# Second-layer softmax of a decoder stack: maxima subtracted by matmul, clamp on ScalarE, transposes by DMA

## The chip, the cores and the metric

The kernel runs on one core of one Trainium2 chip. A core has five engines with their own instruction streams: TensorE (PE in the profile, its weight loads PEld), VectorE (DVE), ScalarE (ACT), GpSimd (POOL) and SyncE (SP), which here issues all DMAs. TensorE writes to PSUM only[...]. The metric is the device time of one execution in microseconds (us), lower is better; "before" is the median of three runs.

## The reference

Four decoder layers run one after the other on 16 sequences of 128 tokens with 256 features, each with attention in 16 heads of 16 features and a feed-forward part. The first layer's attention works over features within a token, the other three over tokens. The second layer is the one whose attention changes; it quantizes queries, keys, values and the softmax weights to 8 bits:

```python
def _fq(x, delta, zp, n_bits):
    xi = _round_ste(x / delta) + zp
    xq = jnp.clip(xi, 0.0, 2.0 ** n_bits - 1.0)
    return (xq - zp) * delta
...
def _attn(x, ctx, wq, wk, wv, wo, bo, dq, dk, dv, dw):
    ...
    sim = jnp.einsum('bhid,bhjd->bhij', _fq(q, dq, 128.0, 8), _fq(k, dk, 128.0, 8)) * SCALE
    attn = jax.nn.softmax(sim, axis=-1)
    out = jnp.einsum('bhij,bhjd->bhid', _fq(attn, dw, 0.0, 8), _fq(v, dv, 128.0, 8))
    out = out.transpose(0, 2, 1, 3).reshape(b, n, D)
    return out @ wo + bo
```

The second layer runs this twice (on itself, then on the context), the third and fourth layers run plain softmax attention twice each:

```python
logits = jnp.einsum("bhqd,bhkd->bhqk", qh, kh) / jnp.sqrt(jnp.float32(depth))
if mask is not None:
    logits = logits + mask * -1000000000.0
attn = jax.nn.softmax(logits, axis=-1)
out = jnp.einsum("bhqk,bhkd->bhqd", attn, vh)
```

## The kernel before

**Tiling and order.** The 16 sequences are cut into 8 groups of two (`GB = 2`), and `group(g)` writes down all steps of all layers for one group. A step is one or a few instructions with the engines that may run them, a price for each, and the blocks that it reads and writes. `Plan.order` then lays all steps of all eight groups out in time by these prices, with all groups alive at once. It gives each block a place in one SBUF arena of 348 units of 512 bytes per partition, chooses the engine where a step has several ways, and emits the instructions in the order of the planned starts. `LEADS` holds one number per group and stage that is added to a step's due level and so sets which group goes first. The order on every engine, SP's queue of DMAs among them, is fixed by this: an instruction that waits holds up all that is behind it on its engine. PSUM is cut into four one-bank blocks (`pw`) and a single four-bank block (`ps`) for scores. Weights are loaded from DRAM by `weight` (L629) into the arena and are shared by the groups that meet them while they are there.

**The second layer's attention.** `quantized_attention` (L1045) makes integer-valued bf16 queries and keys (`qk`) and values (`vz`). `attention` (L886) then runs over the group's two sequences j. `begin(j)` (L1090) issues the scores of all 16 heads into `ps`: eight matmuls of 256 columns (helper line L833), with four 32-row strips of the array at a time. For each half c of the heads (eight heads), `soft` (L1097) then does:

- DVE takes the negated maximum of each row (L1099), and adds it to the scores on the way to SBUF (L1112); ACT takes the exponential in place (L1118). As a second way, which the planner may take, ACT reads PSUM head by head with the maximum as bias and sums on the way (L1103, L1105).
- DVE sums, inverts and scales (L1124 to L1127).
- POOL multiplies each of the eight heads by its factor and adds `MAGIC`, which rounds to a whole number (L1133); DVE clamps at 255, takes `MAGIC` off and writes bf16 (L1137).
- TensorE transposes the eight 128x128 blocks (L905) into PSUM, and ACT or DVE copies them to SBUF (L910, L911).

`out_of` (L1140) multiplies by the values with `products` (L867): 16 bf16 matmuls (L879), four 32-column strips at a time. ACT scales the result with `dwv` (L1143).

**The later layers' attention.** `plain_attention` (L1197) computes the scores twice: once with queries on the partitions, for the maxima only (L1236, or L1246 and L1251 where a mask is added), and once transposed (L1286, helper lines L844 and L833), so that the weights need no transpose. The negated maxima (16 a row, one a head) are split into three bf16 pieces by POOL or DVE (L1261 to L1264), laid into four 128x128 blocks `mq`, transposed by four PE transposes (L1271) and copied to SBUF (L1275). They enter the second scores by four matmuls of 512 columns with the constant `three`, which sums the three pieces (`below`, L1280, through `laid`, L841). Then 16 fp32 matmuls of 128 columns add the scores.

Of the kernel before, what the change touches and what calls it, by code (L numbers as in the profile page):

```python
# [66 lines left out]
SLOTS = {"sm": (64, 46), "row": (128, 12), "pw": (2048, 4), "ps": (8192, 1), "mq": (1024, 4)}  # L67
# [8 lines left out]
    [83, 27, 167, 130, 306, 193, 74, 226, 213, -45, 163, -53, 159, -84, 116, -64, 214, 400, 286, 283],  # L76
    [-69, -856, -114, -260, -60, 57, -165, -14, -2, -22, -386, -90, 144, -71, -260, -59, -586, -159, -213, -106],
    [49, -47, -11, 314, -162, 407, 51, 168, -361, -27, -172, 141, -4, -107, 36, 5, -54, 235, 78, 92],
    [-16, -228, 250, -173, -19, 106, 36, 203, -176, 14, 164, 2, 299, -144, 10, 309, -45, 154, 150, -1],
    [210, 166, 422, 222, 201, 790, 324, 499, 569, 334, 435, 116, 502, 205, 259, 760, 536, 716, 652, 178],  # L80
    [330, 158, 210, 147, 392, 517, 262, 488, 490, 57, 292, 77, 380, 208, 348, 38, 542, 447, 523, 1141],
    [267, 148, 130, 158, 333, 376, 220, 605, 204, -29, 43, 216, 340, 164, 196, 435, 324, 999, 754, 951],
    [288, 156, 593, 320, 407, 313, 255, 389, 233, 323, -30, 86, 440, 164, 213, 583, 372, 760, 452, 550],
# [344 lines left out]
def decoder_stack_kernel(ctx: ExitStack, tc: tile.TileContext, a: dict, out: bass.AP):  # L428
# [19 lines left out]
    G.memset(magic, MAGIC)  # L448

# [46 lines left out]
    three = const.tile([P, P], BF16, tag="three", name="three")  # L496
    mod = const.tile([P, 32], F32, tag="mod", name="mod")
# [28 lines left out]
    def prepare():  # L526
# [5 lines left out]
        def steps_of_quantization():  # L532
# [8 lines left out]
            V.tensor_tensor(dwv, d[:, :, 2], d[:, :, 3], ALU.mult)  # L541

# [6 lines left out]
        def masks():  # L549

            G.tensor_scalar(later[:, 0:1], mod[:, 0:1], -1.0, 1.0, ALU.mult, ALU.add)
            G.tensor_tensor(later[:, 1:2], later[:, 0:1], mod[:, 1:2], ALU.subtract)
            G.tensor_tensor(three, mod[:, 0:1].to_broadcast([P, P]), mod[:, 1:2].to_broadcast([P, P]), ALU.add)
            G.tensor_tensor(three, three, mod[:, 2:3].to_broadcast([P, P]), ALU.add)

            G.tensor_scalar(m1, m1, -1.0e9, 1.0, ALU.mult, ALU.mult)

        step([("POOL", 2.5, masks)], reads=[raw, dl_token], writes=[mask_token], least=110.0)


# [292 lines left out]
    def wide(v):  # L853
        return paired(v).unsqueeze(3).to_broadcast([P, 4, 2, S])

# [11 lines left out]
    def products(eTs, vz, j, po, ones=False):  # L867
# [3 lines left out]
        def issue():  # L871
            for c in range(2):
                for i in range(2):
                    for s in range(4):
                        if ones:
                            lhsT = ones2[:, i, :]
                        else:
                            lhsT = vz.ap()[:, j, 4 * c + s, 2 * i : 2 * i + 2, :].rearrange("p a d -> p (a d)")
                        T.matmul(  # L879
                            po.ap()[32 * s : 32 * s + 32, 2 * ones + c, :], lhsT=lhsT,  # L880
                            rhs=eTs[c].ap()[:, 2 * s + i, :], start=(i == 0), stop=(i == 1),
                        )
# [3 lines left out]
    def attention(x, wo, begin, soft, out_of, vz, dtype, after):  # L886


        plan.enter(after=after, w=1, oT=1, e=2, eT=2, **({"r": 1} if dtype == F32 else {"eb": 1}))
        wo = weight(wo)  # L890
        oT = block("m", [P, 2, NT], role="oT")
        for j in range(GB):
            ps, held = begin(j)
            eTs = []
            for c in range(2):
# [3 lines left out]
                per = 4 if dtype == F32 else 8  # L899
                for q0 in range(0, 8, per):  # L900
                    pt = block("pw", [P, per, S], dtype)

                    def turn(pt=pt, e=e, q0=q0):
                        for q in range(per):
                            T.transpose(pt.ap()[:, q, :], e.ap()[:, q0 + q, :], ident if dtype == F32 else ident_b)  # L905

                    step([("PE", 0.5, turn)], reads=[e], writes=[pt], holds=[eT])
                    step(
                        [
                            ("ACT", 0.6 if dtype == F32 else 1.2, lambda pt=pt, eT=eT, q0=q0: A.copy(eT.ap()[:, q0 : q0 + per, :], pt.ap())),  # L910
                            ("DVE", 0.66 if dtype == F32 else 0.7, lambda pt=pt, eT=eT, q0=q0: V.tensor_copy(eT.ap()[:, q0 : q0 + per, :], pt.ap())),  # L911
                        ],
                        reads=[pt], writes=[(eT, q0)],
                    )
# [130 lines left out]
    def quantized_attention(x, i, hT, kvT):  # L1045
# [44 lines left out]
        def begin(j):  # L1090
# [3 lines left out]
            step([("PE", 0.24, issue, "rows")], reads=[qk], writes=[ps], holds=es[:1])  # L1094
            return ps, es

        def soft(ps, j, c, e):  # L1097
            m, r, bias = small(8), small(8), small(8)
            step([("DVE", 1.22, lambda: V.tensor_reduce(paired(m.ap()), ps.ap()[:, :, c], AX.X, ALU.max, negate=True))], reads=[ps], writes=[m])  # L1099
            along = lambda: taken.eng == "ACT"  # L1100

            def per_head():
                A.activation(bias.ap(), m.ap(), AF.Copy, scale=one(sc))  # L1103
                for q in range(8):
                    A.activation(  # L1105
                        e.ap()[:, q, :], ps.ap()[:, q // 2, c, q % 2], AF.Exp, bias=bias.ap()[:, q : q + 1], scale=one(sc),
# [363 lines left out]
```

## Time and profile before

| | |
|---|---|
| median of 3 runs (lowest to highest) | 1461.03 us (1458.67 to 1462.03) |
| profiled execution | 1458.82 us, its span on the core 1456.7 us |
| granted TensorE clock, mean | 0.993 |
| DMA | 109.67 MB, 75 GB/s over the span |

The time of an execution is its span and some 2 us around it. The page gives for each engine the busy time and its share of the span, and then groups of instructions: source line, engine, operation, what is written and read, shape and count, then the busy time, the mean duration of one in ns, and the idle time of the engine just before them with what ended it. The line of a helper stands for all its callers, so `L833` and `L879` are told apart by shape and type. fp32 matmuls appear as two records each. Matmuls are pipelined: a record lasts longer than the step to the next one's start. The stage-by-stage lines are shown with the prediction; here are the groups of the step by step softmax of the second layer on DVE, ACT and POOL:

```profile
L1133 POOL TENSOR_SCALAR arena<-arena,sm 128x128 f32<-128x128 f32 x512 | 195.9, 403 | 107.7 <-DVE sm L1127 73.4
...
L1099 DVE TENSOR_REDUCE sm<-ps 128x8 f32<-128x1024 f32 x64 | 77.6, 1213 | 9.8 <-PE ps L833 9.5
...
L910 ACT COPY arena<-pw 128x1024 bf16<-128x1024 bf16 x56 | 56.3, 1011 | 41.9 <-PE pw L905 37.2
```

### The profile page before, as it was taken

Reading aid. Unit: us, or ns where it says so; the run is one execution under the profiler, and the core shown is the slowest. Engines: PE = TensorE matmul, PEld = TensorE weight load, DVE = VectorE, ACT = ScalarE, POOL = GpSimd, SP = SyncE. Lnnn points to the kernel's source line nnn. Section 1 sums busy time; section 2 is a strip of 40 time slices with the busy share of each in tenths; the row PEclk is TensorE's granted clock in tenths of the full one; section 3 lists DMA queues with packets and bytes.
Section 4 is the critical chain, followed back from the end, with each engine's and each line's share of the span. In section 5 each row is a group of like instructions: output and inputs, shape, how many; then the busy total and the mean of one; then the engine's idle time right before and its main releaser. Section 6 shows DMA issues by size and latency. Waiting matters only on the chain. (4 is left out here: it accounts for less than half of the span.)

```text
span 1456.7 us, 35756 instructions
## 1 busy us (share of the span) xinstructions
PE 1398.3 (96%) x14771; PEld 1141.3 (78%) x14771; DVE 1010.9 (69%) x1555; ACT 849.7 (58%) x1490; POOL 633.3 (43%) x1415
## 2 busy tenths in 40 slices
PE   8899998999899999899999999999999999999998
PEld 6677887878678888687878777777878888787777
DVE  1665788898988779767764976779478766556431
ACT  4565676766776656565554665657556454445552
POOL 2232857455777446524432542545634234243210
PEclk9999998999999999999999999999999999999999
DMA  6566513412432122112211532211210111100000
GB/s 207 138 171 192 188 48 102 117 34 67 125 90 95 44 67 70 56 52 66 84 38 45 160 101 97 85 55 56 73 45 2 42 38 66 31 31 2 2 9 23
DMA packets 138386, 109.67 MB, mean 75 GB/s; under 512 B 72288, under 2 KB 127472, under 8 KB 138096
## 3 DMA queue, kind: packets, MB, share of 16 engines
q1 hardware_dynamic: 138224, 107.40, 24.5%
q8 instruction: 116, 1.90, 0.5%
q14 instruction: 46, 0.38, 0.1%
HBM read 80.11 MB, written 27.26 MB: 74 GB/s over the span
## 5 line engine op out<-in xcount | busy, mean ns | idle before, releaser
L688 PE MATMUL pw<-arena 128*128 128x256 f32 x2048 | 484.2, 387 | 7.3 <-ACT arena L654 3.1
L675 PE MATMUL pw<-arena 128*128 128x256 f32 x2048 | 480.9, 385 | 7.8 <-ACT arena L663 2.5
L688 PEld LDWEIGHTS pw<-arena 128*128 128x128 f32 x2048 | 383.0, 192 | 68.8 <-issue 9.3
L675 PEld LDWEIGHTS pw<-arena 128*128 128x128 f32 x2048 | 379.2, 191 | 71.0 <-issue 10.0
L1133 POOL TENSOR_SCALAR arena<-arena,sm 128x128 f32<-128x128 f32 x512 | 195.9, 403 | 107.7 <-DVE sm L1127 73.4
L1314 DVE RECIPROCAL arena<-pw 128x256 f32<-128x256 f32 x64 | 112.1, 1752 | 104.0 <-PE pw L879 86.8
L734 POOL TENSOR_TENSOR arena<-arena,rows 128x512 f32<-128x512 f32 x107 | 137.7, 1289 | 89.7 <-ACT arena L721 74.0
L833 PE MATMUL ps<-arena 32*128 32x128 f32 (+2 forms) x3328 | 153.0, 309 | 2.8 <-DVE arena L1112 1.1
L1236 DVE TENSOR_REDUCE sm<-ps 128x16 f32<-128x2048 f32 x48 | 109.6, 2283 | 36.3 <-PE ps L833 33.8
L833 PEld LDWEIGHTS ps<-arena 32*128 32x128 f32 x3072 | 116.1, 186 | 20.4 <-issue 12.0
L696 DVE TENSOR_TENSOR arena<-pw,arena 128x512 f32<-128x512 f32 x88 | 60.3, 685 | 101.2 <-PE pw L688 99.7
L801 ACT ACTIVATE arena<-pw,cols_sb 128x256 f32<-128x256 f32 x184 | 78.0, 472 | 68.3 <-PE pw L675 65.5
L1261 POOL CAST mq<-sm 128x16 bf16<-128x16 f32 x58 | 15.8, 273 | 234.2 <-DVE sm L1236 114.6
L710 POOL TENSOR_SCALAR sm<-sm 128x2 f32<-128x2 f32 x88 | 20.6, 234 | 215.0 <-DVE sm L705 200.1
L721 ACT ACTIVATE arena<-arena,sm,sm 128x256 f32<-128x256 f32 x149 | 83.2, 597 | 49.3 <-POOL sm L714 48.7
L663 ACT ACTIVATE arena<-pw,cols_sb 128x256 f32<-128x256 f32 x140 | 72.7, 563 | 50.5 <-PE pw L647 47.0
L1275 ACT COPY arena<-pw 128x512 bf16<-128x512 bf16 x64 | 37.3, 582 | 84.5 <-PE pw L1271 77.6
L879 PE MATMUL pw<-arena 128*32 128x128 f32 (+1 forms) x2560 | 82.9, 265 | 3.4 <-ACT arena L910 3.0
L1099 DVE TENSOR_REDUCE sm<-ps 128x8 f32<-128x1024 f32 x64 | 77.6, 1213 | 9.8 <-PE ps L833 9.5
L1302 ACT ACTIVATE arena<-ps 128x1024 f32<-128x1024 f32 x64 | 64.1, 1025 | 33.1 <-PE ps L833 30.3
L647 PE MATMUL pw<-ident,arena 128*128 128x128 f32 x416 | 66.8, 286 | 15.1 <-DMA arena<-in_x_dram 5.1
L910 ACT COPY arena<-pw 128x1024 bf16<-128x1024 bf16 x56 | 56.3, 1011 | 41.9 <-PE pw L905 37.2
(142 smaller groups left out, 1993.8 us busy)
## 6 DMA issues: line engine op xcount, KB each, us to landing
arena<-in_L_xattn_ff_w_dram SPq DMA_DIRECT2D x38, 256.0 KB, 3.0
mha<-arena SPq DMA_DIRECT2D x16, 512.0 KB, 4.5
ca<-arena SPq DMA_DIRECT2D x16, 512.0 KB, 3.9
arena<-mha SPq DMA_DIRECT2D x16, 512.0 KB, 4.4
arena<-ca SPq DMA_DIRECT2D x16, 512.0 KB, 4.5
dqkv<-arena SPq DMA_DIRECT2D x8, 768.0 KB, 4.0
arena<-dqkv SPq DMA_DIRECT2D x16, 384.0 KB, 4.3
arena<-in_L_xattn_W_dram SPq DMA_DIRECT2D x24, 256.0 KB, 2.8
```

Of the source, the lines that this page charges most:

```text
L663: ("ACT", 0.54, lambda c=c: A.activation(dst.ap()[:, c, :], ps.ap()[:, c, :], AF.Identity, bias=biases(c), scale=scales(c))),
L675: T.matmul(ps.ap()[:, m, :], lhsT=w.ap()[:, k, m * P : (m + 1) * P], rhs=t.ap()[:, k, :], start=(k == 0), stop=(k == 1),)
L688: T.matmul(ps.ap()[:, j, :], lhsT=lhs(k, j) if lhs else t.ap()[:, k, j * S : (j + 1) * S], rhs=w.ap()[:, k, :], start=start and j + k == 0 ...
L721: ("ACT", 0.6, lambda j=j: A.activation(xh.ap()[:, j, :], x.ap()[:, j, :], AF.Identity, bias=nb.ap()[:, j : j + 1], scale=rstd.ap()[:, j : ...
L734: ("POOL", 1.33, lambda: G.tensor_tensor(dst.ap(), src.ap(), row(name), op)),
L801: "ACT", 0.47, lambda ps=ps, h=h, m=m, bias=bias: A.activation(h.ap()[:, m, :], ps.ap()[:, m, :], func, bias=bias),
L833: T.matmul(ps.ap()[:, s, c] if i is None else ps.ap()[:, s, c, i], lhsT=left(r, c) if i is None else left(r, c, i), rhs=right(r, c), start ...
L879: T.matmul(po.ap()[32 * s : 32 * s + 32, 2 * ones + c, :], lhsT=lhsT, rhs=eTs[c].ap()[:, 2 * s + i, :], start=(i == 0), stop=(i == 1),)
L1099: step([("DVE", 1.22, lambda: V.tensor_reduce(paired(m.ap()), ps.ap()[:, :, c], AX.X, ALU.max, negate=True))], reads=[ps], writes=[m])
L1133: G.tensor_scalar(e.ap()[:, q, :], e.ap()[:, q, :], r.ap()[:, q : q + 1], MAGIC, ALU.mult, ALU.add)
L1236: V.tensor_reduce(m.ap(), ps.ap().rearrange("p s c i k -> p (s c i) k"), AX.X, ALU.max, negate=True)
L1314: step([("DVE", 1.75, lambda po=po, r=r: V.reciprocal(r.ap(), po.ap()[:, 2:4, :]))], reads=[po], writes=[r])
```

## The change

In the second layer the maxima of all 16 heads are taken at once, split into three bf16 pieces, transposed and copied. Then the scores are computed a second time over a base that TensorE lays first: the transposed pieces times the constant `three_of`. ACT takes the exponential of half of this from PSUM in one instruction. After POOL's rounding, ACT computes `relu(MAGIC + 255 - e)`, which is 255 minus the clamped weight, as bf16. A DMA on SP's queue turns all eight blocks. `products` adds, for each weight block, a matmul with the constant `n255` (-255), so that the result is minus the wanted one, and `dwv` is negated. The alternative per-head way is gone.

For the later layers, `split` lays all pieces into one 128x128 block, `turned_maxima` transposes it once, and the copy is of 128 columns. In place of four 512-column matmuls, 16 of 128 columns (four heads f times four strips) stand among the score matmuls, with `three_of` picking head f's pieces. `LEADS` has other numbers, the `mq` slots are smaller, the sections' needs change (`mt=1`, `eb: 2`), and the constants are made at the start. The rest is as before.

```diff
-SLOTS = {... "mq": (1024, 4)}
+SLOTS = {... "mq": (256, 4)}
...
 LEADS = [
-    [83, 27, 167, 130, 306, 193, 74, 226, 213, -45, 163, -53, 159, -84, 116, -64, 214, 400, 286, 283],
+    [-105, -105, 449, 426, 143, 315, -548, 433, 727, -518, -25, 10, 121, -506, -369, -468, 179, -94, -43, -315],
...
+    top = const.tile([P, 1], F32, tag="top", name="top")
+    G.memset(top, MAGIC + 255.0)
+    n255 = const.tile([P, S], BF16, tag="n255", name="n255")
+    G.memset(n255, -255.0)
...
+            V.tensor_scalar(dwv, dwv, -1.0, None, ALU.mult)
...
+            for f in range(4):
+                t = three_of[:, f, :]
+                G.tensor_tensor(t, mod[:, 3 * f : 3 * f + 1].to_broadcast([P, P]), mod[:, 3 * f + 1 : 3 * f + 2].to_broadcast([P, P]), ALU.add)
+                G.tensor_tensor(t, t, mod[:, 3 * f + 2 : 3 * f + 3].to_broadcast([P, P]), ALU.add)
...
-        step([("POOL", 2.5, masks)], reads=[raw, dl_token], writes=[mask_token], least=110.0)
+        step([("POOL", 5.0, masks)], reads=[raw, dl_token], writes=[mask_token], least=75.0)
...
-    def products(eTs, vz, j, po, ones=False):
+    def products(eTs, vz, j, po, ones=False, missing=False):
...
+                    for n in range(1 if ones or not missing else 2):
+                        for s in range(4):
...
+                            T.matmul(
+                                po.ap()[32 * s : 32 * s + 32, 2 * ones + c, :], lhsT=lhsT,
+                                rhs=n255 if n else eTs[c].ap()[:, 2 * s + i, :], start=i == n == 0, stop=i == 1 and n == missing,
+                            )
...
     def attention(x, wo, begin, soft, out_of, vz, dtype, after):
-        plan.enter(after=after, w=1, oT=1, e=2, eT=2, **({"r": 1} if dtype == F32 else {"eb": 1}))
+        plan.enter(after=after, w=1, oT=1, mt=1, e=2, eT=2, **({"r": 1} if dtype == F32 else {"eb": 2}))
...
-                            T.transpose(pt.ap()[:, q, :], e.ap()[:, q0 + q, :], ident if dtype == F32 else ident_b)
-                    step([("PE", 0.5, turn)], reads=[e], writes=[pt], holds=[eT])
...
+                step(
+                    [("SP", 1.2, lambda e=e, eT=eT: nc.sync.dma_start_transpose(out=eT.ap(), in_=e.ap().rearrange("p q k -> p (q k)")), None, 1.0)],
+                    reads=[e], writes=[eT],
+                )
...
         def begin(j):
...
-            step([("PE", 0.24, issue, "rows")], reads=[qk], writes=[ps], holds=es[:1])
+            step([("PE", 0.24, issue, "rows")], reads=[qk], writes=[ps])
+            m, rest, mq = small(16), small(16), block("mq", [P, P], BF16)
+            step(
+                [("DVE", 2.3, lambda ps=ps: V.tensor_reduce(m.ap(), ps.ap().rearrange("p s c i k -> p (s c i) k"), AX.X, ALU.max, negate=True))],
+                reads=[ps], writes=[m],
+            )
+            mt = turned_maxima(m, rest, mq)
+            def less(ps):
+                for s in range(4):
+                    T.matmul(
+                        ps[:, s].rearrange("p c i k -> p (c i k)"), lhsT=mt.ap()[strip(s)],
+                        rhs=three_of[strip(s)].rearrange("p f k -> p (f k)"), start=True, stop=False,
+                    )
+            ps, issue = scores(less, lambda r, c: qT(r, c, tok), lambda r, c: kz(r, c, tok), True)
+            step([("PE", 0.46, issue, "rows")], reads=[qk, mt, mask_token], writes=[ps], holds=es[:1])
...
         def soft(ps, j, c, e):
...
+                [("ACT", 1.15, lambda: A.activation(paired(e.ap()), ps.ap()[:, :, c], AF.Exp, scale=one(sc)), "exp")],
...
-            step([("DVE", 0.76, lambda: V.tensor_scalar(eb.ap(), e.ap(), MAGIC + 255.0, -MAGIC, ALU.min, ALU.add))], reads=[e], writes=[eb])
+            step([("ACT", 1.05, lambda: A.activation(eb.ap(), e.ap(), AF.Relu, bias=top, scale=-1.0))], reads=[e], writes=[eb])
...
+    def turned_maxima(m, rest, mq):
+        def split(eng):
+            piece = lambda n: mq.ap().rearrange("p (s r) -> p s r", r=32)[:, :, 0:12].rearrange("p s (f n) -> p s f n", n=3)[:, :, :, n]
+            four = lambda t: t.ap().rearrange("p (s f) -> p s f", f=4)
+            eng.tensor_copy(piece(0), four(m))
+            eng.tensor_tensor(four(rest), four(m), piece(0), ALU.subtract)
+            eng.tensor_copy(piece(1), four(rest))
+            eng.tensor_tensor(piece(2), four(rest), piece(1), ALU.subtract)
+        step([("DVE", 1.0, lambda: split(V)), ("POOL", 1.25, lambda: split(G))], reads=[m], writes=[rest, mq])
+        pt, mt = block("pw", [P, S], BF16), block("m", [P, S], BF16, role="mt")
+        step([("PE", 0.1, lambda: T.transpose(pt.ap(), mq.ap(), ident_b))], reads=[mq], writes=[pt], holds=[mt])
+        step(
+            [("ACT", 0.32, lambda: A.copy(mt.ap(), pt.ap())), ("DVE", 0.25, lambda: V.tensor_copy(mt.ap(), pt.ap()))],
+            reads=[pt], writes=[mt],
+        )
+        return mt
...
+            mt = turned_maxima(m, rest, mq)
...
+                for f in range(4):
+                    c, i = divmod(f, 2)
+                    for part in (0, 1) if i else (1, 0):
+                        for s in range(4):
+                            r = strip(s)
+                            T.matmul(
+                                pT.ap()[:, s, c, i], lhsT=kz.ap()[r, c, i, tok] if part else three_of[r, f, :],
+                                rhs=qT.ap()[r, c, tok] if part else mt.ap()[r],
+                                start=masked_T is None and part == 1 - i, stop=(f == 3 or masked_T is None) and part == i,
+                            )
```

## The prediction

> **What bounds the kernel now.** I read the busy shares first, then the stretches in time, then the TensorE groups, then who waits for whom.
>
> ```profile
> span 1456.7 us, 35756 instructions
> PE 1398.3 (96%) x14771; PEld 1141.3 (78%) x14771; DVE 1010.9 (69%) x1555; ACT 849.7 (58%) x1490; POOL 633.3 (43%) x1415
> ```
>
> TensorE (PE) is busy for 96% of the span. Matmuls overlap, so this alone proves little; what does is how long it stands still. In stretches of 100 us (columns: length, then busy time and count of PE, PEld, DVE, ACT, POOL, then clock and DMA):
>
> ```profile
> 0.00:100.00 100.00, 84.99 (x685) 70.64 (x686) 43.09 (x108) 56.89 (x133) 27.56 (x55) 0.98 0.63 173
> ...
> 300.00:400.00 100.00, 94.12 (x1075) 77.16 (x1074) 89.54 (x149) 66.67 (x128) 60.47 (x136) 0.98 0.26 80
> ...
> 700.00:800.00 100.00, 97.70 (x1228) 80.97 (x1227) 62.23 (x92) 52.69 (x84) 37.37 (x83) 1.00 0.16 53
> ...
> 1100.00:1200.00 100.00, 99.72 (x1208) 82.71 (x1210) 75.59 (x90) 57.08 (x96) 30.61 (x72) 1.00 0.09 28
> ```
>
> After the first 100 us PE never rests for more than 7 us in 100, and the granted clock is full (0.993 in the mean). DVE comes near a bound only between 200 and 600 us (85 to 90%). The end is thus set by the amount of matmul work; a faster DVE or ACT is worth only some of the 58 us for which PE is idle in all (15 in the first 100 us, 22 between 100 and 600). No long wait of PE is for a weight DMA: the only DMA waits are 7.9 us for x and the context at the start. The groups which the change touches (busy us, mean ns, idle before):
>
> ```profile
> L905 PE MATMUL pw<-ident_b,arena 128*128 128x128 bf16 x512 | 40.2, 222 | 5.2 <-DVE arena L1137 2.6 <-DVE arena L1315 1.1 <-ACT arena L1058 0.9
> L844 PE MATMUL ps<-arena,three 32*128 32x512 bf16 x320 | 31.6, 384 | 2.5 <-DVE sm L1236 2.2 <-ACT arena L1302 0.2
> L1271 PE MATMUL pw<-ident_b,mq 128*128 128x128 bf16 x256 | 25.1, 220 | 2.4 <-DVE mq L1264 1.7 <-POOL mq L1264 0.7
> L879 PE MATMUL pw<-arena 128*32 128x128 bf16 x512 | 13.8, 222 | 3.2 <-ACT arena L910 3.0
> L833 PE MATMUL ps<-arena 32*128 32x256 bf16 x256 | 12.7, 272 | 1.8 <-DVE arena L1112 1.1 <-POOL arena L1068 0.4 <-ACT arena L1302 0.3
> ```
>
> Means of 220 to 384 ns are latencies. What a matmul takes from PE is the time from its start to the next one's start; summed over the trace these are 39.4 us for L905 (77 ns each), 18.8 for L1271 (0.294 us per four), 0.226 us per four of `three`, 18.5 for the bf16 L879 (every fourth 56 ns, the others 3 to 4, since four strips run together), 11.4 for the bf16 L833 (0.356 us per eight). These, not the means, are my prices.
>
> **PE, part by part.** There are 32 batches in the second layer (8 groups, 2 attentions, 2 sequences) and 64 in the two later layers.
>
> - Turns of the weights by DMA: 512 transposes go, -39.4 us.
> - Maxima of the later layers in one transpose: three of four go. A group of four took 0.294, less 3 x 0.056 (the step within a group) leaves 0.126 for one: 64 x 0.126 - 18.8 = -10.7 us.
> - The second layer gains such a transpose: 32 x 0.126 = +4.0 us.
> - Its second scores: four matmuls of 512 columns (0.226) and eight of 256 (0.356): 32 x 0.582 = +18.6 us.
> - Products with `n255`: 16 more matmuls, four rounds of 0.056: 32 x 0.224 = +7.2 us.
> - Later layers: four 512-column matmuls become 16 of 128 columns among the fp32 ones. The trace has no such mixture. Rounds of four fp32 scores start 111 ns apart, with weight loads of 187 ns under way meanwhile; bf16 ones of 128 columns 56 ns apart. Two of the four new rounds come just before an fp32 weight load, which I let set their pace: 2 x 0.056 + 2 x 0.107 = 0.32 us against 0.226, so 64 x 0.096 = +6.1 us. Low end: no extra. High end: each of three additional changes of operand type costs the 0.2 us seen from the last score (903.241 us) to the next full-width matmul (903.441), +38 us. I stay near the low end, since the one change of type in the trace is free: last `three` matmul at 902.236, first fp32 score 217 ns later, just its 512 columns:
>
> ```profile
> 902.23 0.39 PE L844 MATMUL ps<-arena,three 32*128 32x512 bf16 x4
> 902.45 1.06 PE L833 MATMUL ps<-arena 32*128 32x128 f32 x32
> ```
>
> Sum: -39.4 - 10.7 + 4.0 + 18.6 + 7.2 + 6.1 = **-14.2 us** of PE work.
>
> **The other engines.** DVE loses, per half batch, one subtraction (61 x 1.22), the clamp (64 x 0.78) and 8 copies of 0.68; its 64 reductions of 1.21 become 32 of 2.28 (equal), and 11 more splits of 1.47 and a few row additions and diagonal steps fall to it: about -107 us, from 69% to 63%. ACT loses the copies (56.3), the exps from SBUF (69.1), the per-head form (16.5) and 37.3 at L1275; it gains 64 exps from PSUM at 1.11 (the L1302 row with a bias column), 64 Relus at about 1.1 and 90 copies of 128 columns at about 0.27 (from 376 ns for 256 and 582 for 512): about -15 us. POOL gets 21 more splits of 1.06 us and loses seven larger steps: about +6. All these lie beside PE. Their worth is in the 22 us of PE idle between 100 and 600 us; I take **-4 us**, since most of these waits are short and of many kinds.
>
> Here the Trainium skill speaks against one edit: "ScalarE: Activation LUTs", Rules for kernel authors, wants relu, max and min on VectorE. By the rows the clamp costs 0.78 us on DVE and about 1.1 on ACT, so the rule is right for the step alone: 64 x 0.3 = 20 us more engine time. But neither engine sets the end, and DVE is the fuller one where PE idles; by rule or row the sum stays as it is.
>
> **The new chain and its waits.** First scores, reduction 2.28, split 1.06, transpose, copy 0.27, second scores: some 4 us in which PE's next step for this batch waits, and behind it everything in PE's fixed order. The later layers already run exactly this chain; their L1271 waited 2.4 us in 64 batches, so 32 more cost +1.2 us. After the second scores: exp 1.11, sum, reciprocal and scale 1.69, POOL twice 8 x 0.403 (L1133), Relu 1.1: 10.3 us, then the turn. In the built order of PE, other work priced as above stands between a batch's second scores and its products: 18 us in the tightest case, 24 in the next, about 56 in the middle. A landing of up to 8 us is hidden everywhere, one of 14 in all but one case. I add 1 us.
>
> **The turn by DMA** is not in the trace. Nearest rows: loads of the same 256 KB.
>
> ```profile
> arena<-in_L_xattn_ff_w_dram SPq DMA_DIRECT2D x38, 256.0 KB, 3.0
> arena<-in_L_xattn_mha_wv_dram SPq DMA_DIRECT2D x6, 256.0 KB, 4.0
> ```
>
> They hold SP for 0.4 us. Low end 3 us. High end from the skill: "VectorE: DVE Perf Modes", The three transpose paths, gives 390 ns on TensorE and 1309 ns by DMA for 128x128 bf16, and its rules prefer TensorE where PSUM will do. Eight blocks would be 10.5 us, an estimate from that page; held on SP for all of it, 64 x 10.5 = 670 us of queue. The trace's TensorE price is 77 ns, so by the rule this is the worse path by far. I take about 4.5 us to land and 1 to 2 on SP, nearer the row, because that page's figure is for a lone block and its fixed part need not recur eight times. What matters is whose time it is: PE is the bound and is spared 39 us, while SP has room, 382 records at 0.43 = 164 us of issuing in the span. In the built order SP gets 64 turns and 17 fewer weight loads. A turn waits for its Relu, and weight loads queued behind it wait too; SP already stands in waits up to 90 us long without PE ever waiting for a weight, so I cost this at nothing. If that cover goes, the rival below is what happens.
>
> **Sum:** 1458.8 (profiled execution, span 1456.7 and 2.1 around it) - 14.2 - 4 + 1.2 + 1 = 1442.8, say **1442 us**. The median of the three runs, 1461.0, is 2 us above the profiled execution; the forecast is 1.3% below it.
>
> **Rivals.**
> 1. *The order packs better as well* (chance 0.14). PE waits over 0.5 us add up to 46 us, 15 of them in the first 60 us; with DVE down, half of the rest goes: 1442 - 15 = 1427. For it: DVE at 86 to 90% just where PE rests. Against: the waits have over twenty different releasers, DVE's clamp (L1137) alone 2.6 us.
> 2. *PE saves nothing* (0.06): the interleaved fp32 and bf16 scores cost 0.22 us per batch more than priced, 64 x 0.22 = +14: 1442 + 14 = 1456, no change. The free change of type above speaks against it.
> 3. *The turns choke the queue* (0.20), the slower side. Place: SP, between the first and last turn (150 to 1100 us in the old trace), one turn in 15 us. At 10.5 us each they take 670 of 950 us, other issues 105; the remaining 175 must hold all waits for slots and inputs, which today are far more. Weight loads then miss their matmuls: 1.5 us for each pair of turns (most of the 1.9 us step that a weight feeds) gives 32 x 1.5 = 48: 1442 + 48 = 1490. It decides from about 6 us of SP per turn, half of what lies between two turns. For it: fixed order, one queue for all. Against: 3 us rows, and weights that today are never late.
>
> **How the numbers follow.** Forecast 0.60, own range 1430 to 1452 (the score rounds at +0 or +14, idle better or worse by 8). With rival 1 that makes faster 0.74; rival 2 is within 0.2%, about what a measurement of this kernel can tell from no change; rival 3 slower, 0.20. The range of 1424 to 1466 holds the forecast, most of rival 1, rival 2 and the mild end of rival 3.
>
> **What would show it.** PE: no 128x128 bf16 group of 512; about 14 us less start-to-start time, the interleaved rounds near 0.32 us of bf16 per batch. DVE near 63%. The turn: landing near 4.5 us, SP held below 2. No PE or PEld wait put down to weights or turned tiles. Wrong if turns land beyond 10 us, if PE waits for weight DMAs add up to over 10 us, or if PE idle grows from 58 us by more than the work that is saved.

## The result and the profile after

The changed kernel takes 1466.30 us (median of 7 runs, 1465.19 to 1468.25), the kernel before in its 7 runs 1461.03 (1457.88 to 1462.34). The ratio is 1.0048 with a 95% interval of 1.0037 to 1.0059: the change makes it slower by half a per cent, where 1442 us was forecast.

The head of the page after the change, as the first fence of the prediction showed it before:

```profile
span 1465.5 us, 37787 instructions
PE 1403.0 (96%) x15763; PEld 1137.2 (78%) x15763; DVE 898.5 (61%) x1455; ACT 832.6 (57%) x1483; POOL 615.7 (42%) x1502
```

VectorE is rid of 112 us, ScalarE of 17. TensorE, the bound, is busy for 4.7 us longer, in 992 more matmuls, and the span is 8.8 us longer. Stretches of 100 us after the change (length, busy time and count of PE, PEld, DVE, ACT, POOL, then granted clock and DMA):

```profile
200.00:300.00 100.00, 84.98 (x745) 66.60 (x744) 69.03 (x128) 70.50 (x122) 73.55 (x177) 0.91 0.39 100
300.00:400.00 100.00, 96.62 (x856) 76.79 (x855) 67.50 (x123) 66.96 (x119) 60.97 (x158) 0.99 0.48 118
...
600.00:700.00 100.00, 89.65 (x1185) 69.55 (x1185) 71.18 (x107) 54.07 (x90) 51.16 (x130) 0.97 0.30 68
700.00:800.00 100.00, 99.76 (x1164) 81.53 (x1163) 62.99 (x93) 54.18 (x91) 46.09 (x106) 1.00 0.38 112
```

and two of them before it:

```profile
200.00:300.00 100.00, 93.69 (x729) 76.50 (x729) 85.99 (x144) 72.75 (x138) 61.56 (x137) 0.95 0.34 91
...
600.00:700.00 100.00, 97.61 (x1117) 79.47 (x1110) 66.93 (x90) 58.56 (x87) 32.11 (x77) 1.00 0.17 54
```

VectorE is at 67 to 69% between 200 and 400 us, where it was at 86 to 90%. Yet PE stands still for 15.0 us between 200 and 300 us (6.3 before) and for 10.4 between 600 and 700 (2.4 before), and the clock is lower just there: 0.91 against 0.95, and 0.97 against 1.00. In most other stretches PE rests less than before. The rests have moved to other places. GpSimd is fuller there than it was (74% for 62, and 51 for 32), VectorE a little in the second stretch (71% for 67), but no engine beside PE is near full in either.

To compare kernels I split each span in three. **Idle** is the span less PE's busy time, both on the page. **Half clock** is what PE loses while busy in stretches in which the trace grants it a clock of 0.50 (counted as half of its busy time there). **Work** is the rest: busy time at full clock.

| us | span | work | idle | half clock |
|---|---|---|---|---|
| before | 1456.7 | 1389.2 | 58.3 | 9.1 |
| after | 1465.5 | 1386.2 | 62.5 | 16.7 |
| difference | +8.8 | -3.0 | +4.2 | +7.6 |
| in the prediction | -16.0 | -14.2 | -1.8 | 0 |

So there are three errors to explain: 11 us of work that did not go, 6 us of idle time, and 8 us of half clock, a term that the prediction did not have at all.

**Where half clock comes from.** PE's timeline near 278 us (start, duration, then in brackets the idle time before), and the clock in the stretches around:

```profile
269.41 1.06 PE L1017 MATMUL pw<-arena 128*32 128x128 f32 x32
...
277.98 0.62 PE L844 MATMUL ps<-arena 32*128 32x256 bf16 x8 [5.79 <-ACT arena L1114]
...
280.37 1.94 PE L1017 MATMUL pw<-arena 128*32 128x128 f32 x32 [0.73 <-ACT arena L665]
```

```profile
272.00:278.00 6.00, 0.20 (x5) 0.11 (x6) 4.88 (x11) 5.46 (x10) 3.38 (x6) 0.80 0.38 58
278.00:282.40 4.40, 3.67 (x57) 2.71 (x60) 4.23 (x8) 2.17 (x3) 4.16 (x12) 0.50 0.33 61
282.40:290.00 7.60, 7.60 (x75) 6.19 (x66) 6.50 (x15) 6.63 (x12) 6.45 (x20) 1.00 0.34 54
```

PE waits 5.8 us for the exponential that frees the one block of PSUM for scores. What ScalarE does meanwhile, in its own fixed order:

```profile
273.03 1.11 ACT L1114 ACTIVATE arena<-ps,sc 128x1024 f32<-128x1024 f32 x1
274.65 1.09 ACT L732 ACTIVATE arena<-arena,sm,sm 128x256 f32<-128x256 f32 x2 [0.51 <-POOL sm L725]
275.65 1.13 ACT L1133 ACTIVATE arena<-arena,top 128x1024 bf16<-128x1024 f32 x1
276.81 1.11 ACT L1114 ACTIVATE arena<-ps,sc 128x1024 f32<-128x1024 f32 x1
```

Between the exponentials of the two halves stand a normalization and the Relu of another step; this Relu, 1.1 us, is work that the change gave to ScalarE. In the last part of PE's wait the clock drops to half, and it stays there until 282.4 us: the same 32 matmuls of L1017 take 1.94 us in place of 1.06. Within the span, the trace has four such stretches before the change (three of 3.4 us, one of 10.2) and eight after it (3.4 or 6.8 us), besides one at the very end, where PE has nothing left to do. The Trainium skill ("TensorE: Matmul & The Clock Gate", Part 1) says that a monitor looks at windows of about 3.4 us and halves the clock after an idle one, and its table under "Why this matters for your kernels" wants no gaps of PE above about 3 us. The lengths agree. The bound is too mild for this case: of the eight stretches, seven follow 3.4 us in which PE was busy for 26 to 52% (the eighth follows 3.4 us without work), and the longest waits just before or at their start are 2.0 to 5.8 us, five of them below 3. By the rule three waits of the changed kernel would cost half clock; by the trace eight do, and they cost the 16.7 us. Nor is the share of busy time alone the rule: before the change PE was busy for 46% of the 3.4 us from 842.4 us on, and kept the full clock.

### The profile page after: what moved, and what is told of

Same layout as the page of the kernel before. It is cut to its first block, busy times and chain, and to the rows that moved or that the text cites. A ratio compares the mean times of both kernels' runs of the same rounds, so it can differ in the third digit from the quotient of the medians.

```text
span 1465.5 us, 37787 instructions
## 1 busy us (share of the span) xinstructions
PE 1403.0 (96%) x15763; PEld 1137.2 (78%) x15763; DVE 898.5 (61%) x1455; ACT 832.6 (57%) x1483; POOL 615.7 (42%) x1502
## 4 chain that ended last, share of the span: by engine, by line
PE 86%; DVE 6%; ACT 5%; issue 2%; POOL 1%; DMA 0%; SPq 0%; ACTq 0%; DVEq 0%; POOLq 0%
PE pw L686 29%; PE pw L699 29%; PE pw L889 8%; PE ps L1287 6%; PE ps L844 5%; PE pw L658 3%; PE ps L855 2%; DVE sm L1253 1%; ACT arena L960 1%; ACT arena L1308 1%; DVE sm L1119 1%; PE pw L984 1%; POOL arena L1128 1%; DVE sm L1095 1%; PE pw L1017 1%
## 5 line engine op out<-in xcount | busy, mean ns | idle before, releaser
L1128 POOL TENSOR_SCALAR arena<-arena,sm 128x128 f32<-128x128 f32 x512 | 188.9, 391 | 60.5 <-DVE sm L1122 33.6
L745 POOL TENSOR_TENSOR arena<-arena,rows 128x512 f32<-128x512 f32 x103 | 131.3, 1276 | 95.4 <-ACT arena L732 78.1
L1150 POOL CAST mq<-sm 128x16 bf16<-128x16 f32 x79 | 19.2, 243 | 295.3 <-DVE sm L1095 112.2
L1253 DVE TENSOR_REDUCE sm<-ps 128x16 f32<-128x2048 f32 x48 | 109.7, 2284 | 48.2 <-PE ps L844 48.0
L844 PE MATMUL ps<-arena 32*128 32x256 f32 (+1 forms) x1536 | 97.9, 356 | 9.7 <-ACT arena L1114 5.8
L1287 PE MATMUL ps<-arena 32*128 32x128 f32 x2048 | 97.2, 298 | 2.0 <-DVE sm L1253 1.0
L1119 DVE TENSOR_REDUCE sm<-arena 128x8 f32<-128x1024 f32 x64 | 77.5, 1211 | 31.5 <-ACT arena L1114 30.7
L1287 PEld LDWEIGHTS ps<-arena 32*128 32x128 f32 x2048 | 75.7, 187 | 23.5 <-issue 16.6
L889 PE MATMUL pw<-arena 128*32 128x128 f32 (+1 forms) x2560 | 89.0, 267 | 4.7 <-ACT arena L793 3.8
L1133 ACT ACTIVATE arena<-arena,top 128x1024 bf16<-128x1024 f32 x64 | 73.5, 1149 | 31.3 <-POOL arena L1128 25.8
L721 POOL TENSOR_SCALAR sm<-sm 128x2 f32<-128x2 f32 x88 | 17.7, 201 | 174.2 <-DVE sm L716 170.7
L1095 DVE TENSOR_REDUCE sm<-ps 128x16 f32<-128x2048 f32 x32 | 73.0, 2282 | 15.9 <-PE ps L844 15.5
```

The lines of the kernel that those rows point to most:

```text
L745: ("POOL", 1.33, lambda: G.tensor_tensor(dst.ap(), src.ap(), row(name), op)),
L844: T.matmul(ps.ap()[:, s, c] if i is None else ps.ap()[:, s, c, i], lhsT=left(r, c) if i is None else left(r, c, i), rhs=right(r, c), start ...
L889: T.matmul(po.ap()[32 * s : 32 * s + 32, 2 * ones + c, :], lhsT=lhsT, rhs=n255 if n else eTs[c].ap()[:, 2 * s + i, :], start=i == n == 0, ...
L1095: [("DVE", 2.3, lambda ps=ps: V.tensor_reduce(m.ap(), ps.ap().rearrange("p s c i k -> p (s c i) k"), AX.X, ALU.max, negate=True))],
L1119: V.tensor_reduce(r.ap(), e.ap(), AX.X, ALU.add)
L1128: G.tensor_scalar(e.ap()[:, q, :], e.ap()[:, q, :], r.ap()[:, q : q + 1], MAGIC, ALU.mult, ALU.add)
```

## The experiments

All ratios are to the kernel before, timed on the same chip in the same rounds.

**1. The small products issued together.** In the later layers the change puts 128-column bf16 products among the fp32 scores. This version issues the 16 bf16 ones first and the 32 fp32 ones after them:

```diff
-                for f in range(4):
-                    c, i = divmod(f, 2)
-                    for part in (0, 1) if i else (1, 0):
+                for part in (0, 1):
+                    for f in range(4):
+                        c, i = divmod(f, 2)
...
-                                start=masked_T is None and part == 1 - i, stop=(f == 3 or masked_T is None) and part == i,
+                                start=masked_T is None and part == 0 and f == 0, stop=f == 3 and part == 1,
```

> The changed kernel, with the 16 three_of matmuls of a later layer's second scores issued first and the 32 fp32 records after them, nothing else moved on any engine. Work theory (the mixture costs PE time): the block of second scores takes 1.43 us from its start to the next step in the changed kernel and 1.22 in the one before; grouped it falls to about 1.21, 64 x 0.22 = 14 us less, so about 1452 us, ratio 0.994 to the kernel before. Waiting theory (the loss is in waits for the score block and the half clock after them): the time that is freed goes into waits, under 4 us gained, about 1463. Order theory (the planned order itself is worse): the same, about 1463.

Measured: 1459.24 us (1458.04 to 1462.69), ratio 0.9995 (0.9985 to 1.0004). The timeline of one batch in the changed kernel:

```profile
658.25 0.50 PE L1287 MATMUL ps<-arena 32*128 32x128 f32 x8
658.58 0.29 PE L1287 MATMUL ps<-arena,three_of 32*128 32x128 bf16 x8
658.69 0.68 PE L1287 MATMUL ps<-arena 32*128 32x128 f32 x16
659.19 0.29 PE L1287 MATMUL ps<-arena,three_of 32*128 32x128 bf16 x8
659.30 0.46 PE L1287 MATMUL ps<-arena 32*128 32x128 f32 x8
```

and in this version:

```profile
657.13 0.40 PE L1287 MATMUL ps<-arena,three_of 32*128 32x128 bf16 x16
657.37 1.12 PE L1287 MATMUL ps<-arena 32*128 32x128 f32 x32
658.41 1.08 PE L889 MATMUL pw<-arena 128*32 128x128 f32 x32
```

Read the starts; a round is four records, one for each strip of the array. By the medians over the 62 batches at full clock, an fp32 round starts 0.111 us after the one before it and a bf16 round 0.056. Two kinds of round take longer: the fp32 round that begins the block (0.214 us to the next start), and the first fp32 round behind each pair of bf16 rounds (0.165). In the lines this is 0.33 us for the first two fp32 rounds (x8) in place of 0.22, and 0.50 for the four in the middle in place of 0.44. The step from fp32 to bf16 costs nothing extra (0.111). In the kernel before, the first fp32 round stands behind products of 512 columns and takes 0.109; in this version, behind four bf16 rounds, 0.165. From the start of a block to the next step's start, the medians over 64 batches are 1216 ns before the change (226 for the four 512-column matmuls, 990 for the scores), 1434 after it and 1279 here. Interleaving costs 64 x 0.218 = 14.0 us of PE, grouping 64 x 0.063 = 4.0. Grouping does not reach the 1.21 us that was expected of it, so 10 us could go and not 14: the work falls by 9.1 us against the changed kernel (1386.2 to 1377.1), the time by 7.1.

**2. Only the turns by DMA.** The kernel before with the DMA turn in place of transposes and copies, a second eb block, and `LEADS` as they were:

```diff
-                            T.transpose(pt.ap()[:, q, :], e.ap()[:, q0 + q, :], ident if dtype == F32 else ident_b)
...
+                    [("SP", 1.2, lambda e=e, eT=eT: nc.sync.dma_start_transpose(out=eT.ap(), in_=e.ap().rearrange("p q k -> p (q k)")), None, 1.0)],
```

> The kernel before with one part of the change alone: the weights are turned by DMA (two eb blocks, as in the change), all else and LEADS as before. Work theory: the 64 turns took 0.457 us each at full clock, 29 us of PE work goes and nothing comes in its place, so about 1432 us, ratio 0.980; turns land in about 3.1 us as in the changed kernel. Queue theory (turns on SP hold up weights): 1461 or slower, with PE waits put down to weight DMAs.

Measured: 1550.35 us, ratio 1.0611 (1.0594 to 1.0628), with work 1359.0, idle 148.1 and half clock 41.7. PE's work falls by 30.2 us, and the time rises by 90. The turn's own line in this run (min/median/max ns on the queue, then who waited for it):

```profile
L900 SPq DMA_TRANSPOSE arena<-arena x64: 1231/1233/3332, 148.2 to 1242.5; - x64
...
  PE pw L879: 18.9, 6
...
DMA to landing us min/median/max: 3.0/3.1/6.6
```

A turn holds the queue for 1.23 us and lands after 3.1, and still PE waits 18.9 us for turned tiles, six times. The longest of these waits, 8.3 us, ends with a turn that was issued 0.03 us after VectorE had made its input, which was late; the next, 6.9 us, with one that left 2.6 us after its input was there, behind loads, and took 6.6 to land. No wait of PE is for a weight, so the queue theory, which wanted waits for weights, fell too. The remaining idle time has many other names, such as 12.2 us of score steps waiting for L1100 on VectorE. The gain was there, and idle time and half clock together took four times as much (89.8 and 32.6 us more than before).

**3. Turns by DMA, one transpose for the pieces, small products grouped.** The previous one with the change's `turned_maxima` and `three_of` in the later layers; in the second layer the maxima are still subtracted by DVE (60 of 64 half batches) or ACT. `LEADS` is that of the kernel before.

> As e2_turns, and the later layers' maxima in one transpose with the three_of matmuls grouped ahead of the fp32 ones; the second layer keeps its subtraction on VectorE and its clamp on VectorE. Work theory: 29 us of turns and 64 x (0.234 - 0.066) = 11 us of transposes go, the grouped matmuls cost nothing more: about 1421 us, ratio 0.973. Waiting theory: less than half of this, 1441 or slower, since freed PE time turns into waits. Order theory: nothing said about its sign, as LEADS were not made for it.

Measured: 1517.61 us, ratio 1.0390 (1.0374 to 1.0406), with work 1351.4, idle 127.0, half clock 38.9. This is the least work so far, 37.8 us below the kernel before, in a kernel 4% slower. What the changed kernel does beyond this, above all the second scores and the products with `n255`, takes the saving back: its work is 1386.2.

**4. The changed kernel with the old `LEADS`.** Nothing but the table goes back.

> The changed kernel with LEADS of the kernel before, so another order of the same work. Order theory (the new LEADS are the loss): faster than the changed kernel, 1458 or less, ratio under 1.0. Work and waiting theories: the same PE work in an order not made for it, 1470 to 1490, ratio 1.006 to 1.02.

Measured: 1544.78 us, ratio 1.0575 (1.0557 to 1.0594), with work 1391.6, idle 112.1, half clock 39.1. Against the changed kernel only the planner's order differs, and 78 us with it; neither theory had so much. With the order goes the choice of engine where a step has several ways, since the planner makes both; "order" means both from here on. Every comparison of one edit under a table made for something else (2, 3 and 4) measures first of all the table.

**5. and 6. A shorter hold of the score block, and as much relief elsewhere.** PE waits 22.0 us ahead of steps that write the score block, 5.5 before the change. If VectorE's maxima (2.28 us each) hold it too long, halving them should help, and the same relief at other places should not. The first version takes the maxima of 64 of the 96 batches over half of the columns; the second leaves those whole, and takes the second layer's sums and the statistics of the normalizations over half (the last two cuts below).

```diff
-                [("DVE", 2.3, lambda ps=ps: V.tensor_reduce(m.ap(), ps.ap().rearrange("p s c i k -> p (s c i) k"), AX.X, ALU.max, negate=True))],
+                [("DVE", 2.3, lambda ps=ps: V.tensor_reduce(m.ap(), ps.ap().rearrange("p s c i k -> p (s c i) k")[:, :, 0:64], AX.X, ALU.max, negate=True))],
...
-                    V.tensor_reduce(m.ap(), ps.ap().rearrange("p s c i k -> p (s c i) k"), AX.X, ALU.max, negate=True)
+                    k = S if may_be_empty else 64
+                    V.tensor_reduce(m.ap(), ps.ap().rearrange("p s c i k -> p (s c i) k")[:, :, 0:k], AX.X, ALU.max, negate=True)
...
-                V.bn_stats(st.ap()[:, j, :], x.ap()[:, j, :])
+                V.bn_stats(st.ap()[:, j, :], x.ap()[:, j, 0:128])
...
-                V.tensor_reduce(r.ap(), e.ap(), AX.X, ALU.add)
+                V.tensor_reduce(r.ap(), e.ap()[:, :, 0:64], AX.X, ALU.add)
```

> The changed kernel; 64 of the 96 reductions of maxima (all of the second layer's, and those of the two context attentions of the later layers) look at half of each row's columns, so some maxima are not the true ones. Same order on every engine. Each reduction holds the score block ps about 1.1 us less, 64 x 1.1 = 70 us less of DVE and of the block's 840 us. Score-block theory (PE waits because the one block is not free): PE's idle time before score steps falls from 22 us to under 15, and the kernel gains 8 us or more, 1458 or less. Rival (DVE and the chain as a whole are late, whatever they hold): it gains no more than e7_half_elsewhere.

> The changed kernel; the second layer's 64 sums of exponentials and the 176 row statistics of the norms look at half of the columns, so sums and norms are not the true ones. Same order on every engine. About 64 x 0.6 + 176 x 0.13 = 61 us less of DVE, none of it while the score block is held. Score-block theory: PE's idle time before score steps stays above 17 us, and the gain is under 4 us, 1462 or more. Rival (chain as a whole is late): it gains as much as e6_half_maxima or more.

Measured: 1465.27 us, ratio 1.0037 (1.0024 to 1.0050), and 1463.25, ratio 1.0021 (1.0009 to 1.0033). VectorE is down by 64 and 51 us, the waits ahead of the score block still 19.3 and 20.5 us, the time lower by 1 to 3 us in both. The theory fell: neither VectorE's hold of the block nor its load makes most of these waits. The list of waits could have said so: 14.1 of the 22.0 us are put down to exponentials on ScalarE, which also hold the block, and no run shortened those. But an order can remove them: in e10 below, under 2 us of such waits are left.

**7. to 9. Orders searched for the program.** `LEADS` is a table of numbers that shifts when each group's steps are taken; TensorE's instructions stay the same in kind and number. I searched new tables for three programs by the length that the kernel's own planner gives: e8 for number 3 (the planner's price of a turn and of the second scores mended as well), e9 for number 1 (likewise), and e10 for the changed kernel as it is.

> The kernel of e3_turns_one (the kernel before with the turns by DMA, one transpose for the pieces of the maxima and grouped small products; maxima still subtracted by ScalarE) with a new table LEADS, searched offline for this program. The table changes nothing but the order in which the groups' steps are issued. Theory 'the order has to fit the program': TensorE's work stays at e3's 1351 us, its idle time falls from 127 us to some 60 (as in the kernel before and in the change), the half clock's loss from 39 to 10-17 us, and the time is 1423-1435 us, below both kernels. Rival 'a turn by DMA in itself opens gaps': idle stays above 100 us whatever the order and the time above 1490 us. Between them (1435-1490) the order carries part of it, and the idle time before the steps that read turned tiles tells how much.

> The kernel of e1_grouped (the change with the small products issued together) with a new table LEADS searched for it. Work 1377 us as in e1. Theory 'the order has to fit the program': the searched order leaves idle time and half clock at or below e1's 63.6 and 16.2 us, so 1435-1457 us. Rival 'the change's order is as good as orders get, and a plan's length does not carry over to the chip': idle over 75 us and 1465 us or more.

> The changed kernel itself, small products interleaved as in the change, with another searched table LEADS and nothing else changed. Work 1386 us as in the change. If the extra 4 us of idle time and 7.6 us of half clock in the change belong to its particular order and not to what it computes, another order that fits gives 1445-1460 us; if they belong to the new chain of steps (maxima subtracted under a second set of scores), they stay, at 1463 us or more.

| | time (range), us | ratio (95%) | work | idle | half clock |
|---|---|---|---|---|---|
| e8_turns_new_order | 1443.61 (1441.91 to 1445.08) | 0.9885 (0.9867 to 0.9903) | 1348.6 | 73.4 | 19.9 |
| e9_grouped_new_order | 1437.78 (1436.08 to 1438.97) | 0.9845 (0.9830 to 0.9860) | 1379.8 | 48.1 | 9.2 |
| e10_after_new_order | 1448.63 (1446.57 to 1450.33) | 0.9919 (0.9906 to 0.9933) | 1386.1 | 47.3 | 11.3 |

The changed kernel runs at 1448.6 instead of 1466.3 us in another order, and faster than the kernel before. The head of this page (e10):

```profile
span 1444.7 us, 37733 instructions
PE 1397.3 (97%) x15763; PEld 1131.3 (78%) x15763; DVE 904.3 (63%) x1480; ACT 848.3 (59%) x1485; POOL 602.9 (42%) x1489
```

Against the page after the change, PE has the same 15763 matmuls and the same work, 15 us less idle time and 5 us less at half clock. The other engines have more to do together: VectorE 6 us and ScalarE 16 more, GpSimd 13 less. The waits ahead of the score block are down from 22.0 to 9.5 us with its use unchanged. The largest waits of PE after the change, and then in e10 (us in all, times, longest):

```profile
PE ps L844 <- ACT arena L1114: 5.8, 1, 5.8
...
PE ps L855 <- DVE sm L1253: 4.2, 2, 2.2
...
PE ps L844 <- ACT arena L1308: 3.4, 4, 1.3
```

```profile
PE pw L984 <- ACT arena L960: 7.8, 3, 4.5
...
PE ps L1287 <- DVE sm L1253: 3.4, 2, 2.3
...
PE ps L844 <- ACT arena L1114: 1.3, 3, 0.8
```

Single waits of 2 to 6 us come and go at other lines with the order. In e8, with the turns of number 3, idle time falls from 127 to 73 us and the time by 74, though 9 us short of what was expected: the turn by DMA does not of itself open most of the gaps, the order does. What holds the last 25 us of idle time above e9's is not shown. e9, with grouped products and an order made for them, is the fastest of all, 1.55% below the kernel before.

**10. and 11. The kernel before with new orders.** Is the gain of e10 the change's, or only the search's? Two tables for the kernel before, found in the same manner:

> The kernel before with a new table LEADS, searched offline for it in the same way as the tables of e9 and e10; nothing else is changed. The question is what the change is worth when both designs have an order that was searched alike. Theory 'order makes the difference, the change in itself is worth its 3 us of work': work stays at 1389 us, idle falls from 58 to about 48 us and the half clock's loss stays near 10, as in e10, so 1446-1454 us, within 5 us of e10's 1448.6. Rival 'the changed design packs better because VectorE has 107 us less to do': the kernel before cannot be packed much better, idle stays at 55 us or more and the time at 1456 us or above, so that the change is worth 8 us or more once ordered.

> The kernel before with a second other table LEADS, whose planned length lies between that of the kernel before and that of e11. It tells how much two orders of one program differ on the chip. Theory 'order makes the difference': a time between 1446 and 1462 us, different from e11's by several us, with the difference in idle time and half clock and none in work (1389 us). Rival 'orders of nearly equal planned length run alike': within 2 us of e11.

Measured: 1447.61 us (1447.09 to 1449.54), ratio 0.9917 (0.9901 to 0.9932), with work 1385.8, idle 51.2, half clock 10.4; and 1452.85 us (1451.25 to 1454.66), ratio 0.9951 (0.9935 to 0.9967), with 1388.9, 53.1 and 8.9. From the first one's page:

```profile
PE 1396.2 (96%) x14771; PEld 1142.9 (79%) x14771; DVE 1010.9 (70%) x1562; ACT 845.4 (58%) x1477; POOL 630.6 (44%) x1412
```

VectorE has its 1011 us as ever, and still the kernel before packs to within 1 us of the changed one: 0.9917 against 0.9919, each with an interval of about 0.003. The rival, that the change packs better because VectorE is relieved, fell. One program in three orders gives 1461, 1453 and 1448 us. The same yardstick fits the version with grouped products: 0.9845 (e9) against 0.9917 is some 10 us, 6 of them work, so the change without the interleaving does gain 0.7% on the kernel before, once both have an order made for them.

## Why the prediction was wrong

**The sum of PE's work failed first, in two terms.**

- *Turns, "-39.4 us".* This was taken from start to next start over all eight-block turns, and so held PE's waits around them (6.5 us) and half clock (1.9 us) too. The median of a turn at full clock is 457 ns, and 64 of them are 29.3 us; number 2 measured -30.2. A removed matmul does not give back a wait as work.
- *Interleaved small products, "+6.1 us".* Measured 0.444 us per batch for them against 0.226 before, so 64 x 0.218 = +14.0. What the prediction priced came: four bf16 rounds of 0.056, and 0.054 us more behind each of the two pairs of them, where it had let an fp32 weight load set the pace (0.107 in place of 0.056). What it left out is the head of the block. The old 512-column products stood there, and the first fp32 round behind them was free (0.109); the block now begins with fp32 scores, whose first round takes 0.214: 64 x 0.105 = 6.7 us. The trace before had this: the 256-column fp32 scores on L833 take 0.320 us for their first round behind other steps, and 0.216 behind the 512-column products. No change of type from fp32 to bf16 costs anything, so the high end looked at the wrong place.

The others held: the later transposes -10.8 (forecast -10.7), the second layer's transpose +2.1 (+4.0), second scores 32 x 0.554 = +17.7 (+18.6), products with `n255` 32 x 0.223 = +7.1 (+7.2). (The prices 0.294 and 0.356 held waits as well, medians 0.234 and 0.328; in the first these cancelled.) With measured terms the sum is -29.3 - 10.8 + 2.1 + 17.7 + 7.1 + 14.0 = +0.8 us, not -14.2. The split of the spans gives -3.0, and between e11 and e10, the two designs in their new orders, +0.3. As the kernel before alone gives 1385.8 to 1389.2 in three orders, these agree within what an order alone moves: the change saves no work worth naming.

**The order failed second.** "I take -4 us" for idle time was argued from VectorE's load, and half clock was left at nothing without a reason: the mean clock of 0.993, read as full, already stood for 9.1 us. The diff has a whole new table `LEADS`, and I priced each edit as if the rest stood where it had stood. Numbers 2 to 4 show what that assumption is worth: 112 to 148 us of idle time where a table meets another program. The changed kernel's own table fits it, about as well as the old one fitted the old kernel (62.5 and 58.3 us of idle time), but its waits lie closer together and some are longer, with eight stretches of half clock for four: +4.2 and +7.6. In e10 the first and 5.4 of the second are gone with the table alone. That VectorE's load does not decide it is shown from both sides: 112 us less load lowered nothing, 51 to 64 us less again (5 and 6) gave 1 to 3 us, and the kernel before packs nearly as well with all its load (e11).

**What held.** VectorE was forecast at 63% and is at 61%, ScalarE at 15 us less and has 17 less; POOL was forecast 6 us fuller and has 18 less. The turn was taken near the row of a load, not near the rule's estimate of 10.5 us:

```profile
L910 SPq DMA_TRANSPOSE arena<-arena x64: 1231/1238/2290, 186.7 to 1121.3; - x64
...
who waited for it (us, times):
  DVE arena L733: 0.5, 1
...
DMA to landing us min/median/max: 3.0/3.1/4.8
```

It lands in 3.1 us (forecast 4.5) and holds SP for 1.24 (1 to 2); nobody on PE waits for it or for a weight. (SP's issues add up to 262 us, and to 183 before, not 164; there was room.) By the estimate from the figure in the Trainium skill ("VectorE: DVE Perf Modes", The three transpose paths), 10.5 us, it would have been three times as long; no run here times a lone block. So rival 3, the choked queue, fell, and the slower side came from elsewhere. Relu on ScalarE costs 1.149 us (forecast 1.1), as the rule would have it for the step alone. That it does not touch the end, as the prediction said, no run tests by itself; in the 5.8 us wait at 278 us such a Relu is 1.1 us of the chain. The new chain's waits are as small as forecast: the groups of `L1157` and `L1102` waited 0.7 and 2.1 us in all, where +1.2 was added to 2.4.

Rival 2 was nearest, "PE saves nothing", at 1456. Its reason was half of the truth (the interleaved products cost 14 us, though in all and not beyond the 6); the other half, the turns' price, was in none of the cases. The nearness of its number is luck, since idle time and half clock were not in it. Rival 1 named idle time that can be had: e10 has 11 us less of it than the kernel before, but e11, without the change, has 7 less. The prediction's own sign for being wrong, PE's idle time growing by more than the work that is saved, is what came: +4.2 against 3.0.

Left open: why the search for the changed kernel's own table ended where it did, and whether a longer one would part the two designs again by more than the 1 us between e10 and e11. Why the first fp32 round takes longer at the head of a block or behind bf16 rounds is not shown either. Which of the planner's costs misleads it most was not tried either.

## What to carry to other kernels

Where a kernel's order is planned and fixed, an edit and its order are one thing: time the edit under an order made for it, and give the kernel before an order searched as long, or you measure the search (here some 12 us for the kernel before and 18 for the changed one, and 74 to 78 where the table was made for another program). Price what is removed from the bound engine by the median of undisturbed blocks at full clock, never by a sum of start-to-start times that holds waits. And where small bf16 matmuls share a block with fp32 ones, as here, put them together and ahead of the fp32 ones, not among them.

## What the hardware showed that I had not expected

- Half clock needs no long wait. In the kernel before, a stretch of 10.2 us at 0.50 began after 3.4 us in which PE was busy for 54% and never stood still for more than 0.9 us at a time; in number 2, 148 us of idle time came with 42 us lost at half clock.
- Row-tiled matmuls of 128 columns: four bf16 rounds cost 444 ns among fp32 ones and 289 ahead of them (1434 and 1279 less 990 of the fp32 scores alone), against 226 ns for the same product in four matmuls of 512 columns. The loss lies in fp32 rounds: 0.214 us for one that begins the block and 0.165 for one behind bf16 rounds, where others take 0.111.
- A transpose of a 128x1024 bf16 tile from SBUF to SBUF by DMA held the issuing queue for 1.24 us and landed after 3.1, in every kernel that had it; on TensorE the same eight blocks took 0.457 us of PE, besides a copy of 0.7 to 1.0 us.
